# Eleven places for nine in the third pass by half rows, and weights formed between its last units

## The chip, the cores and the metric

One core of a Trainium2 chip runs the whole program. The metric is the device time of one execution in microseconds, as the median of several runs. A profiled execution, taken apart from those, gives the trace; its times run from the first instruction of the span.

## The reference, cut to what matters

Four graph layers follow each other over one adjacency matrix of 2708 x 2708, float32, each added to its input and normalized by rows (`x` is 2708 x 128):

```python
x = _layernorm(x + _L0_gnn_ref(x, adj, ...))
x = _layernorm(x + _L1_gnn_ref(x, adj, L1_gnn_W, L1_gnn_a))
x = _layernorm(x + _L2_gnn_ref(x, adj, ...))
x = _layernorm(x + _L3_gnn_ref(x, adj, ...))
```

The change lies in the second one, an attention layer:

```python
XW = X @ W
s_col = XW @ a[0, :f]
s_row = XW @ a[0, f:]
Z1 = leaky_relu(s_row[:, None] + s_col[None, :], negative_slope=0.01)
den = exp(Z1)
num = A @ den
att = where(num != 0, den / where(num != 0, num, 1.0), 0.0)
H = A @ (att @ XW)
```

An entry of `den` is the larger of two products of a row's factor and a column's factor. When the columns are sorted by `s_col`, a row takes one product up to some column and the other after it. So `num` can be carried along the sorted columns: a start, and then small updates by the rows that change sides.

## The kernel before, in words

The host hands in the transposed adjacency matrix `adjT`. The 2708 rows are 21 tiles of 128 and one of 20. Tiles 0 to 15 are read from memory in every pass; tiles 16 to 20 and the last 20 rows stay on the chip in `res`. A pass multiplies all rows of `adjT` by some weights on TensorE.

Layer 0 takes two passes (the second with the weights `y2`, L1010), with a search for near rows between them. Then comes the **third pass**, the subject here. It forms the starts of the attention sums: for each of 11 chains of blocks two sums over all rows, by the weights `lc` (32 columns, 22 used). Behind it runs the block layer (`block_layer`, L1594): 44 steps, which gather the rows of two blocks each with indirect DMAs on POOL (`load`, L1484), multiply them by the block weights `lw` (`find_num`), invert on ScalarE, correct on VectorE and add up (`add_up`). Layers 2 and 3 follow in `two_layers`.

The third pass goes by half rows. A **unit** (`line` in the code) is one tile of 128 rows by one half of the columns (1354): 677 KB by the profile's account. There are 32: `lines` lists units 0 to 15 for the first half, 16 to 31 for the second. `add_line` (L1328) multiplies a unit in four pieces of 338 or 339 columns into one PSUM bank per half. A resident unit (`own_line`, L1412) does so with a tile of `res`, five for each half, and `add_last_rows` (L1336) with the last 20 rows.

A unit from memory needs a place. `berths` (L1017) lists nine: six in `ring`, which the panels of the second pass used, and three in a pool named `more`. `line_at` (L1022) gives unit n its place, and `load_line` (L1026) issues its load on SyncE's queue:

```python
return berths[n % AHEAD if n < 3 * AHEAD else AHEAD - 3 + n % 3]
```

The first nine units are loaded ahead; in `line` (L1403) the multiplication of unit n is followed by the load of unit n + 9. Units 0 to 26 go round the nine places; units 27 to 31 go to the three of `more`, in turn (27 and 30 where 24 was, 28 and 31 where 25 was, 29 where 26 was).

TensorE has other work in this stretch: it finds the ranks of the columns, the lists of rows in each block, and the block weights. The order of TensorE, VectorE and ScalarE is written out by hand (`tc.manual_schedule`), for this stretch in the list `turns` (L1420). Its items, in the order of the kernel before:

- `blocks_of_edges`, `in_rank_order(0..3)`, `counts`, `ranks_known`: ranks and counts; `ranks_known` issues the first fetches of `xws` on POOL
- `in_list_order(0..3)`: the lists; the last one ends in `listed`, which writes the row numbers `slot_i` for the gathers and starts `lw`
- `next_weights`, six times: `weights` (L1299) turns four columns of `g_col` on TensorE (the last time two) and forms 8 blocks' weights, on VectorE for groups 0, 2, 4, 5 and on ScalarE for groups 1 and 3
- `last_xw` (L1118), a small product that was left over

`end_half` (L1347) copies a half's sums to `heads` and moves them with four DMAs from ScalarE's queue into the tile `carry`, where the block layer's loads pick them up (SyncE, L1495). `carry` takes the memory named "y", which held `y2` in the second pass. At the end SyncE loads the last rows into `res` again (L1432), which waits for `add_last_rows(1)`. The block layer's `load(0)`, `load(1)` and `load(2)` write into strips 0, 1 and 2 of `ring`: strip n is places 2n and 2n + 1.

SyncE's and POOL's order is not written out by hand; the framework places their instructions and all waits.

Of the kernel before, what the change touches and what calls it, by code (L numbers as in the profile page):

```python
# [8 lines left out]
F32 = mybir.dt.float32  # L9
# [7 lines left out]
P = 128  # L17
# [35 lines left out]
def kernel(  # L53
# [17 lines left out]
    N, D = x.shape  # L71
    assert D == P
    T = (N + P - 1) // P
# [8 lines left out]
    S = T - RES  # L82
    NB = (N + BJ - 1) // BJ
    NCH = NB // CH
    NQ = NB // 2
    assert NB == NCH * CH == NQ * 2 and NCH >= 8 and 2 * NCH <= 32 and NB * 2 <= P
    HALF = N // 2
# [8 lines left out]
    def few(c):  # L96
        g = c % GROUPS * 32
        return slice(g, g + LAST)
# [5 lines left out]
    big = ctx.enter_context(tc.tile_pool(name="big", bufs=1))  # L104
# [186 lines left out]
    y = big.tile([P, T, D], F32, tag="y", name="y")  # L291
# [665 lines left out]
    at = due.at  # L957
# [58 lines left out]
    more_pool = more.enter_context(tc.tile_pool(name="more", bufs=3, side="right"))  # L1016
    berths = [ring[:, n * HALF : (n + 1) * HALF] for n in range(2 * STRIPS)]  # L1017
    berths += [more_pool.tile([P, HALF], F32, tag="more", name="more") for _ in range(3)]
    AHEAD = len(berths)
    lines = [(i, h) for h in range(2) for i in range(S)]  # L1020

    def line_at(n):  # L1022

        return berths[n % AHEAD if n < 3 * AHEAD else AHEAD - 3 + n % 3]

    def load_line(n):  # L1026
        i, h = lines[n]
        nc.sync.dma_start(line_at(n), adjT[i * P : (i + 1) * P, h * HALF : (h + 1) * HALF])

    for n in range(AHEAD):  # L1030
        load_line(n)
# [15 lines left out]
    with tc.tile_pool(name="rank", bufs=1) as rank:  # L1047
# [267 lines left out]
            nc.vector.tensor_add(w, w, slot_f[:, b0 : b0 + m, None].to_broadcast([P, m, BJ]))  # L1315
            nc.vector.tensor_scalar_max(w, w, 0.0)

        carry = big.tile([P, NQ * P], F32, tag="y", name="carry")
        edges = [HALF // 4 * g + min(g, HALF % 4) for g in range(5)]
        span = edges[1]  # L1320
        banks = [acc_tile() for _ in range(2)]
# [6 lines left out]
        def add_line(i, h, src, last=False):  # L1328
            for g in range(4):
                nc.tensor.matmul(  # L1330
                    banks[h][32 * g : 32 * g + 32, : edges[g + 1] - edges[g]], lhsT=lc[:, i, :],
                    rhs=src[:, edges[g] : edges[g + 1]], start=(h, g) not in begun, stop=last,
                )
                begun.add((h, g))
# [10 lines left out]
        HEADS = 96  # L1345

        def end_half(h):  # L1347

            tot = heads[:, h * span : (h + 1) * span]
            nc.scalar.copy(tot[:, : edges[4] - edges[3]], banks[h][:, : edges[4] - edges[3]])  # L1350
            nc.scalar.copy(tot[:64, edges[4] - edges[3] :], banks[h][:64, edges[4] - edges[3] : span])
            for g in range(4):
                w = edges[g + 1] - edges[g]
                nc.scalar.dma_start(
                    carry[HEADS : HEADS + 2 * NCH, h * HALF + edges[g] : h * HALF + edges[g + 1]],
                    tot[32 * g : 32 * g + 2 * NCH, :w],
                )

# [44 lines left out]
        def line(n):  # L1403
            for _ in range(n):
                at = loaded[0]
                loaded[0] += 1
                i, h = lines[at]
                add_line(i, h, line_at(at), last=at == 2 * S - 1)
                if at + AHEAD < 2 * S:
                    load_line(at + AHEAD)  # L1410

        def own_line(n):  # L1412
            for _ in range(n):
                h, i = divmod(held[0], FULL - S)
                held[0] += 1
                add_line(S + i, h, res[:, i, h * HALF : (h + 1) * HALF], last=held[0] == FULL - S)
                if held[0] == FULL - S:
                    end_half(0)

        turns = [  # L1420
            (line, 4), (blocks_of_edges,), (line, 5), (own_line, 2), (last_xw,), (in_rank_order, 0), (line, 2),
            (in_rank_order, 1), (line, 2), (in_rank_order, 2), (count_lone,), (line, 2), (counts,), (line, 1),
            (add_last_rows, 0), (own_line, 3), (line, 2), (ranks_known,), (line, 2), (own_line, 1), (in_list_order, 0),
            (line, 2), (in_list_order, 1), (in_list_order, 2), (line, 2), (own_line, 1), (in_list_order, 3), (line, 1),
            (next_weights,), (next_weights,), (line, 1), (own_line, 1), (next_weights,), (line, 2), (next_weights,),
            (own_line, 1), (line, 1), (next_weights,), (line, 1), (next_weights,), (own_line, 1), (add_last_rows, 1),
            (line, 2),
        ]
        for f, *args in turns:
            f(*args)  # L1430
        for c in range(C):
            nc.sync.dma_start(res[few(c), FULL - S, cols[c]], adjT[FULL * P :, cols[c]])  # L1432
        end_half(1)
        assert loaded[0] == 2 * S and held[0] == 2 * (FULL - S) and work["groups"] == 6
        xws, lw = work["xws"], work["lw"]
        order.close()
# [368 lines left out]
```

## Time and profile before

| | |
|---|---|
| median of 3 runs | 1069.48 us (1066.82 to 1074.9) |
| profiled execution | 1089.06 us |
| its span | 1087.3 us |
| TensorE busy | 993.7 us, 91% of the span |
| VectorE, ScalarE, GpSimd busy | 637.1, 331.4, 271.8 us |
| granted clock of TensorE, mean | 0.962 |
| loads of units, first and last issue | 421.5 and 502.5 us |
| first and last multiplication of a unit start | 458.0 and 520.7 us |
| first product of the block layer | 522.7 us |

The parts of the profile to read are the windows (busy time of each engine in a stretch), the timeline of one engine (instructions in order; in brackets how long the engine was idle before one, and what ended that), and the waits of a queue. `acc<-more` or `acc<-ring` at L1330 is the multiplication of a unit, named by its place, `acc<-res` a resident one; a unit shows as eight records. `mis<-ident,g_col` at L1060 is TensorE's part of `next_weights`, `sl<-val_b,hot_in` at L1171 that of `in_list_order`.

### The profile page before, as it was taken

Reading aid. Unit: us, or ns where it says so; the run is one execution under the profiler, and the core shown is the slowest. Engines: PE = TensorE matmul, PEld = TensorE weight load, DVE = VectorE, ACT = ScalarE, POOL = GpSimd, SP = SyncE. Lnnn points to the kernel's source line nnn. Section 1 sums busy time; section 2 is a strip of 40 time slices with the busy share of each in tenths; the row PEclk is TensorE's granted clock in tenths of the full one; section 3 lists DMA queues with packets and bytes.
Section 4 is the critical chain, followed back from the end, with each engine's and each line's share of the span. In section 5 each row is a group of like instructions: output and inputs, shape, how many; then the busy total and the mean of one; then the engine's idle time right before and its main releaser. Section 6 shows DMA issues by size and latency. Waiting matters only on the chain.

```text
span 1087.3 us, 11655 instructions
## 1 busy us (share of the span) xinstructions
PE 993.7 (91%) x3773; PEld 484.8 (45%) x3773; DVE 637.1 (59%) x1358; ACT 331.4 (30%) x609; POOL 271.8 (25%) x339
## 2 busy tenths in 40 slices
PE   0898999999987898796799999999999999999996
PEld 0445544444433455553233333334444644564444
DVE  5885449999934476772599999997121112122122
ACT  0000126555401134601577777664001100010000
POOL 4000000000675563015388644440111100000000
PEclk9889999999998998798899999999999999998998
DMA  9999330000383565498356545556765866574752
GB/s 340 360 330 283 123 116 1 1 0 1 121 275 96 169 186 171 153 375 283 84 144 162 155 133 158 141 138 203 230 204 178 284 201 200 155 265 131 242 161 74
DMA packets 102001, 191.00 MB, mean 176 GB/s; under 512 B 14022, under 2 KB 43342, under 8 KB 101930
## 3 DMA queue, kind: packets, MB, share of 16 engines
q1 hardware_dynamic: 83764, 152.22, 42.3%
q0 software_dynamic: 17728, 37.62, 12.6%
q8 instruction: 32, 0.52, 0.2%
q10 hardware_dynamic: 438, 0.31, 0.1%
q14 instruction: 39, 0.32, 0.1%
HBM read 214.80 MB, written 4.16 MB: 201 GB/s over the span
## 4 chain that ended last, share of the span: by engine, by line
PE 49%; DVE 1%; ACT 1%; issue 1%; DMA 0%; POOL 0%; POOLq 0%; DVEq 0%
PE acc L204 27%; PE num L1609 10%; PE hacc L1467 9%; PE mis L285 1%; PE mis L1740 0%; DVE inv L1456 0%; DVE err L1452 0%; ACT gb L234 0%; PE mis L1706 0%; DVE inv L1459 0%; PE mis L1736 0%; DMA ring<-carry 0%; ACT inv L1442 0%; POOL rstd L253 0%; ACT inv L1445 0%
## 5 line engine op out<-in xcount | busy, mean ns | idle before, releaser
L1488 POOL DMA_INDIRECT ring<-in_adjT,slot_i x88 | 101.0, 1148 | 105.9 <-PE num L1609 81.9
L1609 PE MATMUL num<-ring,lw 128*64 128x512 f32 (+1 forms) x528 | 115.1, 560 | 6.3 <-DVE err L1452 4.1
L1467 PE MATMUL hacc<-inv,xws 128*128 128x512 f32 (+1 forms) x264 | 112.4, 562 | 0.3 <-DVE inv L1459 0.3
L699 PE MATMUL acc<-zT,z 128*128 128x512 f32 (+2 forms) x252 | 102.2, 552 | 0.0
L1442 ACT ACTIVATE inv<-num,plain 128x1024 f32<-128x1024 f32 x88 | 80.6, 916 | 59.4 <-PE num L1609 33.2
L253 POOL TENSOR_TENSOR rstd<-rstd,minus_half 128x4 f32<-128x4 f32 (+1 forms) x18 | 17.3, 961 | 315.1 <-DVE rstd L252 315.1
L234 ACT COPY gb<-acc 128x512 f32<-128x512 f32 (+2 forms) x18 | 9.6, 536 | 252.7 <-PE acc L204 252.7
L700 ACT COPY key<-acc 128x512 f32<-128x512 f32 (+2 forms) x126 | 67.1, 535 | 55.1 <-issue 27.9
L1452 DVE TENSOR_TENSOR err<-inv,num 128x1024 f32<-128x1024 f32 x88 | 74.7, 854 | 14.5 <-ACT inv L1445 12.5
L204 PE MATMUL acc<-ring,y 128*128 128x512 f32 (+2 forms) x192 | 82.5, 560 | 0.5 <-issue 0.5
L1467 PEld LDWEIGHTS hacc<-inv,xws 128*128 128x128 f32 x264 | 46.9, 191 | 78.3 <-issue 48.6
L729 POOL DMA_INDIRECT got<-y_rows,where x66 | 69.9, 1059 | 36.9 <-DVE near_sum L742 17.0
L204 PE MATMUL acc<-ring,xs 128*128 128x512 f32 (+2 forms) x192 | 78.2, 551 | 0.0
L1459 DVE SCALAR_TENSOR_TENSOR inv<-gb,g_inv,inv 128x1024 f32<-128x1024 f32 x88 | 77.0, 914 | 0.1
L204 PE MATMUL acc<-ring,carry 128*128 128x512 f32 (+2 forms) x192 | 74.5, 542 | 0.0
L204 PE MATMUL acc<-ring,m_rows 128*128 128x512 f32 (+2 forms) x192 | 74.3, 542 | 0.0
L1456 DVE SCALAR_TENSOR_TENSOR inv<-err,inv 128x1024 f32<-128x1024 f32 x88 | 72.2, 859 | 0.1
L1445 ACT ACTIVATE inv<-inv 128x1024 f32<-128x1024 f32 x88 | 67.6, 768 | 2.8
L699 PEld LDWEIGHTS acc<-zT,z 128*128 128x128 f32 x252 | 45.8, 190 | 50.4 <-issue 45.0
L575 POOL TENSOR_TENSOR slot_e<-near,sim 128x44 f32<-128x44 f32 (+2 forms) x3 | 0.7, 243 | 267.0 <-DVE d2inv L603 264.9
L1609 PEld LDWEIGHTS num<-ring,lw 128*64 128x64 f32 x528 | 36.1, 138 | 66.6 <-issue 47.2
L701 DVE MAX8 near<-key 128x8 f32<-128x2708 f32 x21 | 62.3, 2965 | 2.7 <-ACT key L700 2.7
(374 smaller groups left out, 1380.0 us busy)
## 6 DMA issues: line engine op xcount, KB each, us to landing
ring<-in_adjT SPq DMA_DIRECT2D x74, 1024.0 KB
ring<-in_adjT SPq DMA_DIRECT2D x17, 768.0 KB
part<-in_adjT SPq DMA_DIRECT2D x12, 1024.0 KB
ring<-in_adjT SPq DMA_DIRECT2D x18, 677.0 KB
more<-in_adjT SPq DMA_DIRECT2D x14, 677.0 KB
ring<-in_adjT SPq DMA_DIRECT2D x17, 552.0 KB
res<-in_adjT SPq DMA_DIRECT2D x4, 1280.0 KB
part<-in_adjT SPq DMA_DIRECT2D x3, 768.0 KB
```

The source lines that it names most:

```text
L204: nc.tensor.matmul(accs[c][: lhsT.shape[-1], :w], lhsT=lhsT, rhs=src, start=start, stop=stop)
L699: nc.tensor.matmul(pks[c][:p, : cw[c]], lhsT=z2[:, :p], rhs=zT[:, cs], start=False, stop=True)
L700: nc.scalar.copy(key[:p, cs], pks[c][:p, : cw[c]])
L729: nc.gpsimd.indirect_dma_start(out=got[:p, :], out_offset=None, in_=y2_rows[:, :], in_offset=bass.IndirectOffsetOnAxis(ap=where[:p, t, k : ...
L1442: nc.scalar.activation(inv, num[:, :w], AF.Ln, scale=plain[:, 0:1], bias=plain[:, 1:2])
L1445: nc.scalar.activation(inv, inv, AF.Exp, scale=-1.0)
L1452: nc.vector.tensor_mul(err, inv, num[:, :w])
L1456: nc.vector.scalar_tensor_tensor(inv, err, 2.0, inv, op0=ALU.subtract, op1=ALU.mult)
L1459: nc.vector.scalar_tensor_tensor(inv, gb[:, col : col + w], g_inv[:, q : q + 1], inv, op0=ALU.max, op1=ALU.mult)
L1467: nc.tensor.matmul(haccs[:, o:e], lhsT=xws[:, q, :], rhs=inv[:, o:e], start=(q == 0), stop=(q == NQ - 1))
L1488: nc.gpsimd.indirect_dma_start(out=rows[i][:KC, n, :], out_offset=None, in_=adj_half[:, :], in_offset=bass.IndirectOffsetOnAxis(ap=slot_i[ ...
L1609: nc.tensor.matmul(num[n * (BJ + 2) : (n + 1) * (BJ + 2), o:e], lhsT=lw[:, 2 * q + n, :], rhs=rows[i][:, n, c0 + o : c0 + e], start=True, ...
```

## The change

Two places are added, in the memory that `y2` leaves ("y", named `y_place`), so eleven units are loaded ahead. These two are used once, by units 9 and 10: `carry`, which takes the same memory, is now made at the first call of `end_half`.

The place of each unit is written as a list, `stays`. Units 0 to 10 take places 0 to 10, 11 to 19 take 0 to 8, 20 to 23 take 0 to 3, 24 to 28 take 4 to 8, and 29 to 31 take 4, 5, 6. `follows` says for each unit which unit comes next in its place; that one's load is issued right behind its multiplication. So unit 20 follows 11, 24 follows 15, 28 follows 19, and units 29, 30 and 31 follow 24, 25 and 26; behind units 9, 10, 20 to 23 and 27 on, no load is issued.

In `turns` two more units stand at the start (4 and 7 for 4 and 5). Fewer stand between the parts of `in_list_order`, so that unit 23 comes just behind the last of them. `add_last_rows(1)` moves from near the end to behind unit 23. The six calls of `next_weights` stand between units 23 and 27, with one resident unit between each two or so, and the last five units stand at the end together.

```diff
+    y_place = big.tile([P, T * D], F32, tag="y", name="y_place")
+    berths += [y_place[:, n * HALF : (n + 1) * HALF] for n in range(2)]
     AHEAD = len(berths)
     lines = [(i, h) for h in range(2) for i in range(S)]
+    stays = [*range(AHEAD), *range(AHEAD - 2), *range(4)]
+    while len(stays) < len(lines):
+        stays.append(4 + (len(stays) - 2 * AHEAD - 2) % (AHEAD - 6))
+    follows = {max(m for m in range(n) if stays[m] == stays[n]): n for n in range(AHEAD, len(lines))}
...
-        return berths[n % AHEAD if n < 3 * AHEAD else AHEAD - 3 + n % 3]
+        return berths[stays[n]]
...
-        carry = big.tile([P, NQ * P], F32, tag="y", name="carry")
+        carries = []
...
+            if not carries:
+                carries.append(big.tile([P, NQ * P], F32, tag="y", name="carry"))
...
-                if at + AHEAD < 2 * S:
-                    load_line(at + AHEAD)
+                if at in follows:
+                    load_line(follows[at])
...
-            (line, 4), (blocks_of_edges,), (line, 5), (own_line, 2), (last_xw,), (in_rank_order, 0), (line, 2),
+            (line, 4), (blocks_of_edges,), (line, 7), (own_line, 2), (last_xw,), (in_rank_order, 0), (line, 2),
             (in_rank_order, 1), (line, 2), (in_rank_order, 2), (count_lone,), (line, 2), (counts,), (line, 1),
-            (add_last_rows, 0), (own_line, 3), (line, 2), (ranks_known,), (line, 2), (own_line, 1), (in_list_order, 0),
-            (line, 2), (in_list_order, 1), (in_list_order, 2), (line, 2), (own_line, 1), (in_list_order, 3), (line, 1),
-            (next_weights,), (next_weights,), (line, 1), (own_line, 1), (next_weights,), (line, 2), (next_weights,),
-            (own_line, 1), (line, 1), (next_weights,), (line, 1), (next_weights,), (own_line, 1), (add_last_rows, 1),
-            (line, 2),
+            (add_last_rows, 0), (own_line, 3), (line, 2), (ranks_known,), (line, 1), (own_line, 1), (in_list_order, 0),
+            (line, 1), (in_list_order, 1), (in_list_order, 2), (line, 1), (own_line, 1), (in_list_order, 3),
+            (line, 1), (add_last_rows, 1), (next_weights,), (own_line, 1), (next_weights,), (line, 1), (next_weights,),
+            (own_line, 1), (next_weights,), (line, 1), (next_weights,), (own_line, 1), (line, 1), (next_weights,),
+            (line, 5),
...
+        carry = carries[0]
```

More of the change, by code (lines that the diff above doesn't have):

```diff
@@ L1018 @@
     berths += [more_pool.tile([P, HALF], F32, tag="more", name="more") for _ in range(3)]
+    y_place = big.tile([P, T * D], F32, tag="y", name="y_place")
+    berths += [y_place[:, n * HALF : (n + 1) * HALF] for n in range(2)]
     AHEAD = len(berths)
     lines = [(i, h) for h in range(2) for i in range(S)]
+    stays = [*range(AHEAD), *range(AHEAD - 2), *range(4)]
+    while len(stays) < len(lines):
+        stays.append(4 + (len(stays) - 2 * AHEAD - 2) % (AHEAD - 6))
+    follows = {max(m for m in range(n) if stays[m] == stays[n]): n for n in range(AHEAD, len(lines))}
+    assert list(follows) == sorted(follows)
     def line_at(n):
-        return berths[n % AHEAD if n < 3 * AHEAD else AHEAD - 3 + n % 3]
+        return berths[stays[n]]
     def load_line(n):
@@ L1354, in end_half @@
                 nc.scalar.dma_start(
-                    carry[HEADS : HEADS + 2 * NCH, h * HALF + edges[g] : h * HALF + edges[g + 1]],
+                    carries[0][HEADS : HEADS + 2 * NCH, h * HALF + edges[g] : h * HALF + edges[g + 1]],
                     tot[32 * g : 32 * g + 2 * NCH, :w],
```

## The prediction

> **What bounds the kernel now.** I read the chain of waits first: over the whole span it is TensorE with hardly a break, except around 500 us, in the third pass by half rows. So I cut that stretch into windows (columns: stretch, length, then busy us and instruction count of PE, PEld, DVE, ACT, POOL; granted clock, DMA share, GB/s).
>
> ```profile
> 448.00:460.00 12.00, 9.75 (x105) 7.52 (x109) 10.75 (x29) 7.65 (x15) 0.28 (x1) 0.53 0.01 5
> 460.00:486.00 26.00, 24.96 (x256) 13.04 (x248) 19.41 (x50) 1.95 (x9) 1.72 (x3) 0.93 0.99 397
> 486.00:490.00 4.00, 4.00 (x42) 2.72 (x43) 2.87 (x5) 0.33 (x2) 2.59 (x2) 1.00 0.40 106
> 490.00:500.00 10.00, 8.14 (x76) 5.29 (x75) 1.66 (x7) 0.00 (x0) 6.03 (x6) 1.00 0.97 369
> 500.00:512.00 12.00, 3.40 (x20) 1.93 (x24) 1.85 (x4) 1.33 (x5) 7.34 (x7) 0.57 1.04 299
> 512.00:521.00 9.00, 9.00 (x102) 3.38 (x94) 4.70 (x10) 3.60 (x12) 0.00 (x0) 1.00 0.16 39
> ```
>
> TensorE is full up to 498.9, works 3.4 of the 12 us from 500 to 512, and is full again. The DMA engines rest where TensorE works (448 to 460) and are full where it waits. Its timeline says on what:
>
> ```profile
> 498.56 0.37 PE L1171 MATMUL sl<-val_b,hot_in 20*128 20x132 f32 x1 [0.44 <-issue]
> 507.42 1.35 PE L1330 MATMUL acc<-more,lc 128*32 128x339 f32 x8 [8.49 <-DMA more<-in_adjT]
> 508.71 1.93 PE L1060 MATMUL mis<-ident,g_col 128*128 128x128 f32 x8
> 511.81 0.78 PE L1330 MATMUL acc<-more,lc 128*32 128x339 f32 x8 [1.17 <-DMA more<-in_adjT]
> 512.40 0.75 PE L1330 MATMUL acc<-res,lc 128*32 128x339 f32 x8
> 513.08 0.65 PE L1060 MATMUL mis<-ident,g_col 128*128 128x128 f32 x4
> 513.66 1.34 PE L1330 MATMUL acc<-more,lc 128*32 128x339 f32 x16
> ...
> 519.14 0.77 PE L1340 MATMUL acc<-res,lc 20*32 20x339 f32 x8
> 519.85 1.34 PE L1330 MATMUL acc<-more,lc 128*32 128x339 f32 x16
> ```
>
> A unit is eight of these records. Counted from unit 0 at 458.03, the one at 507.42 is unit 24, the one at 511.81 unit 25. SyncE's timeline, in a wide and a narrow window, and then its queue's waits from 455 to 525 (total, times, longest):
>
> ```profile
> 488.74 14.13 SPq L1028 DMA_DIRECT2D more<-in_adjT  x8
> 502.54 0.33 SPq L1028 DMA_DIRECT2D more<-in_adjT  x1
> ```
>
> ```profile
> SPq L1432 <- PE acc L1340: 15.1, 1, 15.1
> SPq L1028 <- DMA more<-in_adjT: 11.0, 5, 2.8
> SPq L1028 <- DMA carry<-heads: 6.4, 1, 6.4
> ```
>
> All eight loads 24 to 31 are out by 502.87, before unit 24 is multiplied at 507.42. That is the key. By `line_at`, units 24, 27 and 30 share one place, 25, 28 and 31 a second. Load n+9 is written into the program at unit n, so loads 27 and 30 stand **ahead** of the multiplication of unit 24. They wait for each other's landing (the five waits for `more`), and the multiplication waits for load 30 and reads what came last. So unit 24 stands until load 30 has landed (507.4), and unit 25 until load 31 has (511.8). Behind unit 24 on TensorE's queue stand all six groups of weights.
>
> **What the Trainium skill says.** "DMA: Bandwidth & Descriptors", section on queues, rings and completion order: each engine takes turns between the queues that have work. The trace agrees: from 500 the gathers of POOL come in beside the loads, and the rate falls from 397 to 299 GB/s at a full share. The same page, section on the anatomy of one DMA, prices a GpSimd DMA at 2.0 us plus bytes over 436 GB/s. For 693 KB that is an estimate of 3.6 us, which I use as the least that a load of SyncE takes; no row here shows it alone. "TensorE: Matmul & The Clock Gate", part 1: after an idle window the clock is halved. The trace agrees: 0.57 from 500 to 512, and unit 24 alone took 1.35 us, as much as two units at 513.66.
>
> **The change, part by part.**
>
> *Two more places.* Units 9 and 10 load ahead. The last multiplication from `y2` starts at 438.8 and the loads of units 6 to 8 are issued from 440.1 to 442.5, so these two go out at about 442.5 and use the rest from 448 (1.39 MB at 397 GB/s: 3.5 us). On TensorE they only move: up to 486 it waits for no load worth naming, so ahead of 498 the gain is nothing. If the places came free late, the 3.5 us would fall on a DMA stretch that TensorE doesn't wait for: again nothing, unless over 10 us late.
>
> *The carry tile.* Taken at the end of half 0 instead of earlier; it waits for unit 10, multiplied some 20 us before. Nothing.
>
> *Order up to `in_list_order(3)`.* The same pieces, but 23 units ahead of its end and not 24, at 0.65 us (1.34 for two, less overlap): it ends at 498.93 - 0.65 = 498.3. Units 20 to 23 are loaded when 11 to 14 have been multiplied (about 472 to 477) and needed from 488. Loads 24 to 28 may wait for ACT's four copies of half 0, whose completion semaphores SyncE's loads take in turn (the 6.4 us above). Two units earlier on TensorE put those copies 1.25 us later; load 24 then goes out at about 490, and 24 to 28 land from 494 to 502. They are needed at 501.5, 504, 506, 507 and 507.6. Covered, by 5 us at the end.
>
> *After it.* From the rows: unit 0.65, resident unit 0.68 (512.40 to 513.08), group of weights 0.6 (513.08 to 513.66), last rows 0.71 (519.14 to 519.85). By the new order: unit 23 (0.65), last rows (0.71), group, resident, group (1.88), unit 24: **502.2**. Group, resident, group, unit 25 (2.53): **504.7**. Group, resident, unit 26 (1.93): **506.65**. A short group (0.35), five units (3.25): **510.25**, if nothing is late. VectorE's group takes 1.8 us (0.67 + 0.67 + 0.42), ACT's 2.5, against over 2.4 us from one group to the next but one on the same engine and three `mis` buffers: no wait. `listed` is done at 499.4, ahead of the first group's product.
>
> *Loads 29 to 31: the wait that is added.* They now wait for units 24, 25, 26, so they go out at 502.2, 504.7, 506.65. What is late next is load 31. Free end: 506.65 + 3.6 = 510.25. Crowded end: load 31 of before was issued at 502.54 and waited for until 511.81, 9.2 us, so 515.9. Between: from 500 to 521 before moved 299 x 12 + 39 x 9 = 3.94 MB, of which loads 29 to 31 and the rest of 28 about 2.6, so six gathers 1.35. After: load 2 of the block layer goes into a place that unit 30 still holds, so only four gathers run beside the loads (0.9 MB), with 2.08 for 29 to 31 and 0.7 of unit 28: 3.7 MB from 500 at 299 GB/s, done at **512.3**. I take that for load 31, and 513.0 for the end of unit 31. Before it was 519.85 + 1.34 = 521.2. **Gain 8.2 us.**
>
> *Queued behind.* SyncE: after load 31, the six small loads of `res` and the block layer's `carry` rows; the last `res` load waited 15.1 us for the last rows, which now come at 499.6, so this shrinks and is no path. POOL: the two gathers of load 2 wait for unit 30 (about 511.5, before 506.83 for the sixth gather), then 1.35 each and some 5 us to land: about 519. Its product was at 531.67, 10.5 us after the end of unit 31, so needed at 523.5; it decides from a landing 4.5 us later. ACT: from `heads` (521.26) through four copies and the table load to `inv` (527.61) 6.35 us; all moves with unit 31. The rest is the same work on a full TensorE.
>
> Sum: the profiled execution of 1089.06 us (span 1087.3) would give 1080.9. It stands 19.6 us, 1.8%, over the median 1069.48; scaled, the gain is 8.0 us: **1061.4, say 1061**.
>
> **Rivals.**
> 1. *TensorE sets the end.* The gathers hardly hold the loads; unit 31 ends at about 511. For it: load 31 is then the only one in the queue. Against it: the full share from 490 to 512. Gain 10.2: 1059.
> 2. *Full crowding.* 9.2 us again for load 31: 516.6, gain 4.6: 1065. For it: the same gathers run. Against it: two fewer, and load 31 of before had two loads ahead.
> 3. *Slower: the last three loads become the bound.* They are tied to multiplications that they didn't wait for, and start when POOL's gathers already fill the queues. The end is later than before once load 31 lands after 520.5, 13.9 us after its issue. At twice the crowded latency (18.4) it lands at 525.0: 4.5 us lost, 1074. Against it: no load took so long, and the gathers in its way are fewer.
> 4. *The gain is given back in the block layer.* Load 2 lands at 527 instead of 519 and TensorE stands 3.5 us there: gain 4.7, 1065.
> 5. *The change doesn't do what it says.* The places of `y2` come free late, or hold nothing early: by the working above the time stays 1061.
>
> **How the numbers follow.** The forecast, with rival 5, has 0.60 (1057 to 1065 with run-to-run differences as in the shown runs); rival 1 0.17, rival 2 0.12, rival 3 0.06, rival 4 0.05. The range 1055 to 1068 takes in rivals 1, 2 and 4. One per cent is 10.7 us, about what a measurement can tell from no change: faster by more needs rival 1 and a good draw, or the low edge of the forecast, 0.24; slower by more only a bad case of rival 3, with what I can't see, 0.06; within, 0.70.
>
> **What would show it.** Right: no idle of 8 us before a unit on TensorE near 499; unit 24 right behind a group of weights at about 502; a wait of about 2 us for a load only before unit 31 (or 29, 30); `heads` of half 1 at about 513; a steady block layer behind it. Wrong: a long wait for a load from `ring` between 500 and 520, a wait before unit 9 or 20, or the first steps of the block layer waiting for a gather.

## The result, and the profile after

The kernel after takes 1065.38 us (median of 14 runs, 1061.04 to 1073.66), the kernel before 1072.07 us in the same comparison (14 runs, 1066.82 to 1075.52). The ratio is 0.9935, with a 95% interval from 0.9913 to 0.9956: 7.0 us of 1072 (4.7 to 9.3), where 8.0 were forecast. It is less than one per cent, and its interval lies clear of no change.

The two profiled executions can't be compared as wholes: their spans are 1087.3 and 1061.4 us, but 15.6 of those 25.9 us lie ahead of the first unit (458.03 against 442.42 us), where TensorE has the same work in both. What can be compared is the stretch from the start of unit 0 to the end of unit 31, called **the stretch** from here on. It took 63.2 us before (458.03 to 521.19) and 56.6 us after (442.42 to 499.04): **6.5 us less**, close to the measured 7.0. Each of these two stretches comes from one execution; the last 3.7 of the 25.9 us lie behind unit 31.

The windows of the kernel after, cut at the same distances from unit 0 as those of before in the prediction (columns: stretch, length, busy us and count of PE, PEld, DVE, ACT, POOL, then granted clock, DMA share, GB/s):

```profile
432.40:444.40 12.00, 9.75 (x105) 7.53 (x109) 10.74 (x29) 7.63 (x15) 0.28 (x1) 0.52 0.20 82
444.40:470.40 26.00, 24.96 (x279) 13.35 (x267) 19.41 (x50) 1.95 (x9) 1.72 (x3) 1.00 1.00 396
470.40:474.40 4.00, 3.96 (x42) 2.51 (x41) 3.27 (x6) 0.33 (x2) 2.96 (x2) 1.00 0.42 122
474.40:484.40 10.00, 10.00 (x98) 6.00 (x92) 3.29 (x10) 0.92 (x4) 7.87 (x8) 1.00 0.71 255
484.40:496.40 12.00, 7.28 (x77) 2.65 (x75) 4.75 (x10) 4.01 (x14) 3.23 (x4) 0.94 0.97 261
496.40:505.40 9.00, 4.71 (x17) 2.19 (x19) 0.00 (x0) 1.77 (x3) 2.09 (x2) 0.51 0.32 83
```

Where TensorE worked 8.14 us of ten it now works all ten, and in the next twelve 7.28 us against 3.40. The first row shows a part of the two additional loads: 82 GB/s in 12 us where there were 5. TensorE's timeline around the end of the pass:

```profile
480.10 0.78 PE L1337 MATMUL acc<-ring,lc 128*32 128x339 f32 x8
...
483.37 0.78 PE L1337 MATMUL acc<-ring,lc 128*32 128x339 f32 x8
...
490.03 0.75 PE L1337 MATMUL acc<-ring,lc 128*32 128x339 f32 x8
494.48 0.90 PE L1337 MATMUL acc<-ring,lc 128*32 128x339 f32 x8 [3.71 <-DMA ring<-in_adjT]
497.69 1.35 PE L1337 MATMUL acc<-more,lc 128*32 128x339 f32 x8 [2.31 <-SPq L1811]
502.04 5.94 PE L1619 MATMUL num<-ring,lw 128*64 128x512 f32 x20 [3.00 <-DMA ring<-carry]
```

Unit 23 (480.10) and unit 24 (483.37) come without a wait. The wait has moved to unit 30 (494.48) and unit 31 (497.69): 6.0 us together, where units 24 and 25 had waited 9.7. The bracket of unit 31 names SyncE (L1811), because SyncE itself waits there for the same load 31. SyncE's timeline, in two windows, has the issues:

```profile
484.21 2.90 SPq L1035 DMA_DIRECT2D ring<-in_adjT  x2
488.64 0.33 SPq L1035 DMA_DIRECT2D more<-in_adjT  x1
```

Loads 29 and 30 start at 484.21 and 486.78 (the end of the first row, less 0.33 for one issue), load 31 at 488.64. So unit 30 is used 7.7 us and unit 31 9.0 us after its issue. ScalarE behind it:

```profile
499.12 0.44 ACT L1359 COPY heads<-acc 128x338 f32<-128x338 f32 x1 [10.60 <-PE acc L1337]
...
499.64 3.23 ACTq L1363 DMA_DIRECT2D carry<-heads  x4
503.88 1.28 ACT L1609 ACT_TABLE_LOAD   x1 [4.27 <-SPq L1811]
505.74 1.21 ACT L1452 ACTIVATE inv<-num,plain 128x1024 f32<-128x1024 f32 x1 [0.58 <-DMA ring<-carry]
```

From `heads` to the first inversion it is 6.6 us, against 6.35 before: this piece moved with little change.

### The profile page after: what moved, and what is told of

The parts are those of the page before. It is cut to its first block, busy times and chain, and to the rows that moved or that the text cites. A ratio compares the mean times of both kernels' runs of the same rounds, so it can differ in the third digit from the quotient of the medians.

```text
span 1061.4 us, 11655 instructions
## 1 busy us (share of the span) xinstructions
PE 984.6 (93%) x3773; PEld 482.9 (45%) x3773; DVE 637.0 (60%) x1358; ACT 331.5 (31%) x609; POOL 275.1 (26%) x339
## 4 chain that ended last, share of the span: by engine, by line
PE 48%; DMA 1%; DVE 1%; ACT 1%; issue 1%; POOL 0%; POOLq 0%; DVEq 0%
PE acc L204 28%; PE num L1619 9%; PE hacc L1477 9%; PE mis L285 1%; DMA ring<-carry 1%; DMA ring<-in_adjT,slot_i 0%; PE mis L1750 0%; DVE inv L1466 0%; DVE err L1462 0%; ACT gb L234 0%; PE mis L1716 0%; DVE inv L1469 0%; PE mis L1746 0%; ACT inv L1452 0%; POOL rstd L253 0%
## 5 line engine op out<-in xcount | busy, mean ns | idle before, releaser
L1498 POOL DMA_INDIRECT ring<-in_adjT,slot_i x88 | 104.4, 1187 | 95.9 <-PE num L1619 67.0
L699 PEld LDWEIGHTS acc<-zT,z 128*128 128x128 f32 x252 | 45.8, 190 | 50.4 <-issue 45.0
```

Source lines behind the costliest of these rows:

```text
L699: nc.tensor.matmul(pks[c][:p, : cw[c]], lhsT=z2[:, :p], rhs=zT[:, cs], start=False, stop=True)
L1498: nc.gpsimd.indirect_dma_start(out=rows[i][:KC, n, :], out_offset=None, in_=adj_half[:, :], in_offset=bass.IndirectOffsetOnAxis(ap=slot_i[ ...
```

## The experiments

Each ratio is to the kernel before on the same chip. e1 to e4 shared one chip (before took 1072.91 us there), e5 to e8 a second (1091.15), r1 to r3 a third (1090.13). The stretch is from one profiled execution of each, so it can carry differences that the ratio, from many runs, doesn't show.

| run | what it is | stretch, us | ratio (95%) |
|---|---|---|---|
| before | nine places, last five units in three of them | 63.2 | 1 |
| e1 | before, loads tied to the units that free their places | 62.1 | 0.9983 (0.9969 to 0.9997) |
| e5 | nine places, last ten units in five of them, before's order | 57.5 | 0.9967 (0.9943 to 0.9991) |
| e3 | after's places, before's order | 54.7 | 0.9913 (0.9889 to 0.9937) |
| e2 | after without the two places of `y2` | 57.4 | 0.9936 (0.9916 to 0.9956) |
| after | | 56.6 | 0.9935 (0.9913 to 0.9956) |
| r1 | after again | 56.5 | 0.9952 (0.9932 to 0.9972) |
| e4 | after, units 24 to 26 ahead of the weights | 50.4 | 0.9894 (0.9863 to 0.9926) |
| r2 | e4 again | 60.0 | 0.9905 (0.9878 to 0.9932) |
| e7 | e4 with nine places | 53.6 | 0.9927 (0.9907 to 0.9947) |
| e8 | e4, late copies of the second half's sums | 50.6 | 0.9866 (0.9817 to 0.9916) |
| r3 | e8 again | 51.3 | 0.9878 (0.9847 to 0.9909) |
| e6 | after, first gathers of the block layer left out | 53.8 | one run, no ratio |

### e1: before, with each late load tied to its place

```diff
+    stays = [n % AHEAD if n < 3 * AHEAD else AHEAD - 3 + n % 3 for n in range(len(lines))]
+    follows = {max(m for m in range(n) if stays[m] == stays[n]): n for n in range(AHEAD, len(lines))}
...
-                if at + AHEAD < 2 * S:
-                    load_line(at + AHEAD)
+                if at in follows:
+                    load_line(follows[at])
```

> The kernel before, with its nine places and its order, but each of the last five loads issued behind the multiplication of the unit that holds its place (27 behind 24, 28 behind 25, and so on). From the start of unit 0 to the end of unit 31 the profiled run of before took 63.2 us and that of after 56.6. Theory (the gain is that unit 24 no longer stands behind the loads of later units): no wait of 8 us before unit 24, but units 27, 30, 31 wait for loads tied to 24, 27, 28; 59 to 61 us, ratio to before about 0.997. Rival (the gain is from the two more places and the moved weights): within 1 us of before, 62 to 65 us, ratio 0.999 to 1.002.

The stretch took 62.1 us: over the theory's 61 and just inside the rival's 62 to 65. The ratio, 0.9983, lies between the two. The wait before unit 24 is gone, but waiting comes back further on. TensorE's timeline of e1 (the rows are units 28, 29 and 31; unit 27 waited 0.57 us):

```profile
492.95 1.35 PE L1332 MATMUL acc<-more,lc 128*32 128x339 f32 x8 [3.11 <-DMA more<-in_adjT]
...
495.28 1.36 PE L1332 MATMUL acc<-more,lc 128*32 128x339 f32 x8
...
504.00 1.35 PE L1332 MATMUL acc<-more,lc 128*32 128x339 f32 x8 [3.84 <-SPq L1803]
```

With three places for eight units, loads 27 to 29 wait for units 24 to 26, and loads 30 and 31 for 27 and 28. Two generations of loads stand one behind the other at the end. So setting the loads behind their units is worth about 1 us of the stretch alone; with three places the waiting only moves.

### e5: five places for the last units, and nothing else

```diff
-    stays = [*range(AHEAD), *range(AHEAD - 2), *range(4)]
+    stays = [*range(AHEAD), *range(AHEAD), *range(4)]
...
-        stays.append(4 + (len(stays) - 2 * AHEAD - 2) % (AHEAD - 6))
+        stays.append(4 + (len(stays) - 2 * AHEAD - 4) % (AHEAD - 4))
```

It is after without `y_place`, with these lines, and with before's `turns`.

> Nine places, the last ten units in places 4 to 8 as in e2, and before's order of turns: of the change only the five places for the last units are left (and loads behind the multiplication that frees the place). Theory (five places in the stead of three carry the gain; order and the places of y2 are worth 1 us each way): stretch from unit 0 to the end of unit 31 of 54.5 to 57 us against 63.2 before and 62.1 in e1, ratio to before 0.991 to 0.995. Rival (the two places of y2 are needed with the old order): 59 us or more, ratio 0.996 or above.

57.5 us, half a microsecond over the upper end, and a ratio of 0.9967, which is the rival's (0.996 or above). Against e1 the five places take 4.6 us off the stretch. The times don't confirm that size: the ratios of e1 and e5 are 0.0016 apart, less than 2 us, and their intervals overlap. With before's order the two places of `y2` are worth something, as e3 shows.

### e3: after's eleven places, before's order

> After's eleven places with before's order of turns. Theory (the places carry the gain; units 24, 25, 26 come behind in_list_order(3) with two, one and two groups of weights between, so loads 29 to 31 go out about a microsecond earlier than in after): 55 to 57.5 us for the stretch, ratio 0.992 to 0.996. Rival (weights between the last units carry the gain): 60 us or more, with the last groups of weights late for the block layer, ratio 0.997 or above.

54.7 us and 0.9913, both a little better than expected, and less than the kernel after. TensorE's timeline of e3 at units 30 and 31:

```profile
493.61 0.78 PE L1337 MATMUL acc<-ring,lc 128*32 128x339 f32 x8
497.56 1.35 PE L1337 MATMUL acc<-more,lc 128*32 128x339 f32 x8 [3.18 <-SPq L1811]
```

Unit 30 doesn't wait, unit 31 waits 3.18 us. In before's order units 24, 25 and 26 come 1.3 to 2.2 us sooner than in after's, relative to unit 0, and loads 29, 30 and 31 with them (40.4, 42.2, 44.0 us from unit 0 against 41.8, 44.4, 46.2). So the order of weights between the last units costs the change about 2 us of the stretch; the ratios (0.9913 and 0.9935) agree in sign, but their intervals overlap.

Between e5 and e3 only the two places of `y2` differ, and here the times speak: 0.9967 and 0.9913, with intervals that don't overlap, though on two chips. With nine places loads 27 and 28 must wait for units 22 and 23 and go out at 40.5 and 41.0 us from unit 0; with eleven they follow units 18 and 19 and go out at 34.0 and 34.5. In e5 the last five loads thus start within 6 us, and units 29, 30 and 31 wait 1.27, 0.75 and 2.94 us.

### e2: after without the two places

The diff is that of e5, and `turns` stays as in after.

> After without the two places of y2: nine units ahead, units 9 to 17 in places 0 to 8, 18 to 21 in 0 to 3, the last ten in places 4 to 8. Theory (TensorE waited for no load ahead of unit 24, so two more loads ahead are worth nothing): 56 to 58 us for the stretch, ratio to before 0.993 to 0.996, as after. Rival (the two units ahead carry the gain): 60 us or more, ratio 0.997 or above, with waits for loads among units 9 to 23.

57.4 us and 0.9936: with after's order the two units ahead are worth 0.8 us of the stretch and nothing in the time.

### e4 and e7: units 24 to 26 ahead of the weights

```diff
-            (line, 1), (add_last_rows, 1), (next_weights,), (own_line, 1), (next_weights,), (line, 1), (next_weights,),
-            (own_line, 1), (next_weights,), (line, 1), (next_weights,), (own_line, 1), (line, 1), (next_weights,),
+            (line, 4), (add_last_rows, 1), (next_weights,), (own_line, 1), (next_weights,), (next_weights,),
+            (own_line, 1), (next_weights,), (next_weights,), (own_line, 1), (next_weights,),
             (line, 5),
```

> After with units 24, 25, 26 right behind unit 23, ahead of the six groups of weights, so that loads 29, 30, 31 go out about 1.4 to 6 us earlier. Theory (what is left in after is the latency of the last loads, 9 us from issue under the gathers, behind the multiplications they are tied to): the waits of 3.7 and 2.3 us before units 30 and 31 go or shrink under 1 us, stretch 50.5 to 52.5 us, ratio to before 0.987 to 0.990. Rival (the DMA engines are the bound whatever the order, by the gathers): stretch 55 us or more, as after.

The ratio of 0.9894 is as expected, and 50.4 us a little under the range. TensorE's timeline of e4: units 23 to 25, unit 26, units 29 and 30, and unit 31:

```profile
484.24 1.91 PE L1337 MATMUL acc<-ring,lc 128*32 128x339 f32 x24
485.98 0.74 PE L1337 MATMUL acc<-more,lc 128*32 128x339 f32 x8
...
493.61 1.32 PE L1337 MATMUL acc<-ring,lc 128*32 128x339 f32 x16
496.20 0.78 PE L1337 MATMUL acc<-more,lc 128*32 128x339 f32 x8 [1.28 <-SPq L1811]
```

The loads take as long as in after (load 31 is issued at 486.85 and used 9.35 us later), but they start 5.9 us sooner from unit 0 (40.3 against 46.2 us), and the weights run while they come. 1.28 us of waiting is left of 6.0, where under 1 was expected.

e7 is e4 with the places of e2.

> e4 (units 24 to 26 ahead of the weights) with nine places as in e2. Theory (the places of y2 do nothing here either): stretch 50 to 52 us as in e4 (50.4), ratio to before 0.987 to 0.993. Rival (with the loads freed earlier, units 24 to 28 are now late without the two units ahead): a wait of over 1 us before one of units 24 to 29, stretch 53 us or more.

53.6 us, and the wait before unit 31 is 1.20 us as in e4. The 3.2 us lie elsewhere: a group of weights waits 1.57 us for VectorE, and unit 27 starts 49.1 us from unit 0 against 45.9 in e4. The expectation of 50 to 52 us failed, and so did the rival's, since none of units 24 to 29 waits over 1 us for a load. e4's 45.9 is not typical either: e8 and r3 below, with eleven places and this order, have 47.4 and 48.1. The intervals of e4 and e7 overlap, so what the two places do here is not settled.

### e6: the first gathers left out

```diff
+            if i > 1:
                 nc.gpsimd.indirect_dma_start(
```

> After without the indirect gathers of the block layer's steps 0 and 1 (this part of the computation is left out: those steps multiply what lies in the ring). Theory (the 7.7 and 9 us from issue to use of loads 30 and 31 are the gathers' crowding): load 30 and 31 are used 4 to 5 us after issue, the waits before units 30 and 31 fall from 6.0 us together to under 2.5, stretch 51.5 to 53.5 us. Rival (the latency is that of three loads one behind the other on the loads' own queue): still 7 to 9 us, stretch 55.5 to 57 us.

53.8 us, from one run. TensorE's timeline of e6, then SyncE's, in its two windows:

```profile
506.18 1.51 PE L1337 MATMUL acc<-ring,lc 128*32 128x339 f32 x16
510.51 1.32 PE L1337 MATMUL acc<-more,lc 128*32 128x339 f32 x8 [2.83 <-SPq L1812]
```

```profile
500.35 2.90 SPq L1035 DMA_DIRECT2D ring<-in_adjT  x2
504.78 0.33 SPq L1035 DMA_DIRECT2D more<-in_adjT  x1
```

Units 29 and 30 (506.18) don't wait at all. Unit 31 waits 2.83 us, and is used 5.7 us after its issue in place of 9.0. So the crowding by these four gathers is 3.2 of the 6.0 us of waiting in after. The rest stays without them: load 31 starts with unit 26, and TensorE has less left to do than the load takes. The waits and the stretch are each 0.3 us over their expected ranges, and load 31 took 5.7 us where 4 to 5 were expected.

### e8: the second half's copies out of ScalarE's way

```diff
-                nc.scalar.dma_start(
+                queue.dma_start(
...
+                    if i == 3:
+                        move_half(1, nc.sync)
```

It is e4, with the four copies in a function `move_half`; half 1's sums wait in the memory of `m_rows` until SyncE moves them in step 3 of the block layer, which needs them in step 22.

> e4 with the four copies of half 1's sums into carry issued by SyncE in the block layer's step 3, not by ScalarE right behind unit 31. Theory (ScalarE's 6.4 to 7.3 us from heads to the first inversion set the start of the block layer, of which the copies take 3.2): first hacc product 2 to 3 us sooner behind the end of unit 31 than in e4 (14.3 us), ratio to before 0.984 to 0.990. Rival (the carry rows from SyncE and the first products set it, 3.5 us behind unit 31): under 1 us sooner, ratio as e4.

The first product of `add_up` starts 10.1 us behind unit 31, against 14.3 in e4: 4.2 us sooner, more than the 2 to 3 expected. The ratio, 0.9866, is within its range.

But the edit moved more than ScalarE's copies. In e4 SyncE waited 6.1 us for load 31 before its row loads for the block layer, which start at 496.25, 0.7 us ahead of the end of unit 31 (496.98). SyncE, TensorE and ScalarE of e4:

```profile
496.25 6.92 SPq L1505 DMA_DIRECT2D ring<-carry  x6
500.51 6.99 PE L1619 MATMUL num<-ring,lw 128*64 128x512 f32 x20 [3.53 <-DMA ring<-carry]
504.39 1.21 ACT L1452 ACTIVATE inv<-num,plain 128x1024 f32<-128x1024 f32 x1 [1.30 <-PE num L1619]
```

In e8 the row loads start 6.3 us ahead of the end of unit 31 (509.47). SyncE of e8:

```profile
503.12 6.99 SPq L1513 DMA_DIRECT2D ring<-carry  x6
```

In e4 the first inversion's last wait is for a product (1.30 us), not for ScalarE's own copies, so taking the copies away alone would have brought nothing there. That product had waited 3.53 us for its rows and ran at half clock (0.50 from 499.14 to 505.97); in e8 the first product waits 1.05 us, and the clock is 1.00 from 500 to 520. Earlier products alone would have brought no more than the 1.30 us, since ScalarE was ready only at 503.09, 6.1 us behind unit 31. In e8 the inversion starts 3.2 us behind it, in e4 7.4. So the 4.2 us needed both.

### r1, r2, r3: after, e4 and e8 on one chip

> The kernel after once more, on one chip with r2 and r3. Theory (the gain is the shortened third pass): stretch from unit 0 to the end of unit 31 of 56 to 57.5 us, with 3 to 4 and 2 to 3 us of waiting before units 30 and 31, ratio 0.992 to 0.996. Rival (the waits of the profiled run were a chance of the gathers in that run): waits under 3 us together or over 9.

> e4 once more. Theory (the last loads' latency bounds after): stretch 50 to 51.5 us, 5 to 6.5 us below r1, ratio 0.987 to 0.991. Rival (the block layer gives it back): stretch as expected, ratio no lower than r1's by 0.002.

> e8 once more. Theory (ScalarE's path behind unit 31 sets the start of the block layer): first hacc product 10 to 11 us behind the end of unit 31 against 14 in r2, ratio lower than r2's by 0.003 to 0.006, 0.982 to 0.987. Rival (carry rows set it; the 10.1 us of e8 was a chance): 12.5 us or more, ratio within 0.002 of r2's.

r1 has waits of 4.07 and 1.28 us before units 30 and 31, 5.3 together: the wait is no chance of one run, though its split differs. In r2 the stretch is 60.0 us, far off the expectation, while its ratio of 0.9905 is within it, and 0.0047 under r1's (the two intervals just touch, at 0.9932): the block layer doesn't give the gain back. The windows of r2 say why the stretch is long (TensorE's clock is the third figure from the end):

```profile
472.00:477.00 5.00, 5.00 (x32) 3.22 (x28) 3.98 (x10) 0.00 (x0) 0.00 (x0) 0.50 1.03 418
...
482.00:487.00 5.00, 5.00 (x27) 1.99 (x27) 0.00 (x0) 0.16 (x1) 0.00 (x0) 0.50 0.81 252
```

For 15 us a TensorE that shows no idle time ran at half its clock; this profiled stretch says nothing about the order. Unit 31 waits 0.74 us there. r3 has the first product of `add_up` at 10.1 us again (14.8 in r2). ScalarE's timeline of r3:

```profile
509.32 0.44 ACT L1361 COPY m_rows<-acc 128x338 f32<-128x338 f32 x1 [1.92 <-PE acc L1337]
...
512.02 1.21 ACT L1460 ACTIVATE inv<-num,plain 128x1024 f32<-128x1024 f32 x1 [0.78 <-PE num L1627]
```

From the copy to the inversion it is 2.7 us in place of 6.6 in after; as in e4 and r2, a product ends the last wait. The ratio, 0.9878, lies over the expected 0.982 to 0.987, and its step from r2 (0.0027) just under the expected 0.003; the intervals of r2 and r3 overlap. Its profile supports e8's order; its time alone doesn't separate it from e4. Both r3 and e8 are clear of before, and their median ratios are the lowest of all runs; r3's interval ends at 0.9909, under the lower end of r1's at 0.9932.

## Why the prediction was right, point by point

**What bounded the kernel.** Right. Unit 24 stood behind loads 30 and 31, and the stall is gone. e1 adds what the prediction didn't separate: taking those loads from ahead of the unit is worth 1 us only, as long as three places must serve for eight units. By the stretch the five places are the larger part (e5, 4.6 us less than e1). By the times the division is open: e5 has about half of the gain (0.9967), and e2, with five places and the new order, has all of it (0.9936), but their intervals overlap.

**Up to `in_list_order(3)`.** It was to end 40.3 us from unit 0 (498.3 less 458.03) and ended at 37.7. Two things that the prediction took over from the kernel before make up the 2.5 us. First, 1.2 us are in the last records of this piece. e1, with before's order, runs within 0.1 us of before up to 38.3 us from unit 0, but ends at 39.7 and not 40.9: in before three of these records waited 0.12, 0.23 and 0.44 us (the last is the row at 498.56), with nothing named that ended the waits. Second, in before and e1 the clock was half for 3.4 us from about 11.4 us behind unit 0 (0.50 in e1 from 454.58 to 458.00). Two units took 2.48 us there in e1 and 1.34 in after. That is about the other 1.3 us. All four profiled runs with before's order have this half clock, and eight of the nine with after's order don't; why is not shown.

**From there to unit 26.** 8.35 us predicted, 8.3 measured (480.17 to 488.5). VectorE and ScalarE didn't hold up TensorE, as forecast. Loads 24 and 25 went out at 22.1 and 23.8 us from unit 0, not at 32: only 26 to 28 waited for ScalarE's copies of half 0 (6.5 us in SyncE's waits), and none was late.

**Load 31.** The mechanism was right: the wait moves to the last loads, which are now tied to units 24 to 26. The size was off. Its issue came 2.4 us earlier than predicted, counted from unit 0 (46.2 against 48.6), but it took 9.0 us and not the 5.65 that the sum took (512.3 less 506.65). That is near the crowded end, rival 2's price of 9.2. The sum had four gathers beside the loads and 299 GB/s. There were five, and the rate was 261 GB/s from 484.40 to 496.40. Step 2 of the block layer takes the places of units 29 and 30, so its first gather waits for unit 29 only and went out in the middle of load 31. POOL's timeline of after:

```profile
491.12 1.04 POOL L1498 DMA_INDIRECT ring<-in_adjT,slot_i  x1 [3.91 <-PE acc L1337]
```

What this fifth gather cost alone is not shown; without the four ahead of it, and with both of step 2 in its time, load 31 took 5.7 us (e6).

The two errors have opposite signs, and that the landing came only 1.0 us late (55.3 against 54.3 from unit 0) is luck. Issued when forecast, a load of 9.0 us would have been used at 57.7, and unit 31 would have ended at 59.0: a gain of about 4 us (an estimate from these numbers). The waits also came out larger: 6.0 us before units 30 and 31, where about 2 were forecast. The prediction named a long wait for a load from `ring` here as a sign of being wrong. Unit 30's 3.71 us is one, and the gain came all the same.

**Unit 31 itself.** 0.65 us predicted, 1.35 measured. Behind the wait of 3.7 us the clock was half again (0.51 from 496.40 to 505.40), the very effect that the prediction quoted for unit 24 (Trainium skill, "TensorE: Matmul & The Clock Gate", part 1) and didn't apply to the unit that would wait next. With the 1.0 us of the landing this is the difference: 55.0 us predicted for the stretch, 56.6 measured, so a gain of 6.5 us and not 8.2. Of the 4.4 us between the forecast of 1061 and the measured 1065.38, 2.6 are not the change's: before itself took 1072.07 us in the comparison, not 1069.48.

**The two more places, costed at nothing.** Right with after's order (e2: 0.9936 beside 0.9935). It doesn't hold in general: with before's order e3's stretch is 2.8 us under e5's, and its ratio is clear of e5's.

**The order of the weights.** The prediction counted it as it stood and never asked what another order would give. e3 shows that it costs about 2 us of the stretch by issuing loads 29 to 31 later, and e4 that the opposite order takes 6 us more off it. The ratios agree in sign (0.9894 against 0.9935, 0.9905 against 0.9952), but the first two intervals overlap and the others touch.

**What was queued behind.** ScalarE's piece moved with unit 31 (6.6 us for 6.35). SyncE was through its small loads early and then waited for load 31 before the first `carry` rows (6.3 us in its waits), which TensorE shows as 3.0 us before the first product. ScalarE was ready at 505.16 and waited 0.58 us more for that product's rows, so it cost little. The gathers of step 2 cost no visible wait; the one wait for rows in the first steps is 0.85 us for `carry` at 516.66. Rivals 3, 4 and 5 didn't come about.

## What to carry to other kernels

Where a buffer is used again, ask which instruction its next load waits for, and put that one as early as its own data allows; work that needs no load belongs behind it, to cover the load's latency. Price a load that is issued late by what it takes among the traffic of that moment, not by its bytes. Count half a clock for the first work behind a wait of some 3 us: unit 31 took 1.35 us behind 3.18 us in e3, and 0.78 behind 1.28 us in e4. Then look at what stands behind the last item on the engines that the next stage needs first: here row loads behind a load on SyncE, and on ScalarE four small copies that were needed some 20 steps later.

## What the runs showed of the hardware that was not expected

- TensorE's clock was granted at half for 15 us while its timeline shows no idle time (r2, 472 to 487 us), and one run of the same kernel had 1.00 there (e4). Just ahead of it, up to 469.2, stand three short waits of 0.35, 0.41 and 0.27 us; e4 has the same three. A single profiled stretch can be 9 us off by this alone.
- A load of 677 KB took 9.0 us from issue to use with four gathers of the block layer issued ahead of it and a fifth in its time (after). It took 5.7 us with those four left out and two later ones in its time (e6).
